# A mixture-of-experts layer: units of four and two token tiles, seven block products in two layers, W1 and W3 fetched per unit

## The chip, the core and the metric

The kernel runs on one core of a Trainium2 chip. A core has five engines that run side by side, each through its own list of instructions in program order, and wait for each other through semaphores: TensorE (matmuls, PE in the profile; PEld is its loading of weights), VectorE (DVE), ScalarE (ACT), GpSimd (POOL, which here issues indirect DMAs) and SyncE (SP, which issues the other DMAs). SBUF is the working memory with 128 partitions, PSUM holds what matmuls accumulate in eight banks, and HBM is the memory outside. The metric is the device time of one execution in microseconds (us). The trace is that of one profiled execution.

## The reference

4096 tokens of 256 numbers each go through a layer of eight experts, of which each token uses the two with the largest gate.

```python
var = jnp.mean(x * x, axis=-1, keepdims=True)
xn = rms_w * (x * jax.lax.rsqrt(var + EPS))
gate = xn @ wg_W + wg_b + (genre_embed @ gg_W + gg_b)
gate_w = jax.nn.softmax(gate, axis=-1)
topk_w, topk_i = jax.lax.top_k(gate_w, TOP_K)
cw = jnp.sum(jax.nn.one_hot(topk_i, E, dtype=x.dtype) * topk_w[..., None], axis=-2)
h1 = jax.nn.relu(jnp.einsum('bsh,ehm->bsem', x, W1) + b1)
h2 = jax.nn.relu(jnp.einsum('bsem,emn->bsen', h1, W2) + b2)
out_e = jnp.einsum('bsen,enh->bseh', h2, W3) + b3
return jnp.einsum('bseh,bse->bsh', out_e, cw)
```

The result is added to x. Everything is 32-bit floating point; W1 is 256 x 512, W2 512 x 512 and W3 512 x 256 for each expert.

## The kernel before

The pairs of a token and one of its experts are sorted into tiles of 128 pairs that share an expert. The first eight tiles (E = 8) hold tokens of the first quarter, one tile for each expert, known early; the rest are placed once the gates of all tokens are known. Of the rest 56 are sure to be there (NSURE), and up to 69 are possible (NREST); these inputs have 59. A *unit* is what one step of the loop works on. Units 0 to 7 are single tiles. Then come 24 units of two tiles with a common expert (NPAIRED), then the single tiles that are left over, of which the last run in a branch that is chosen by the count at run time.

A unit has three layers. For a single tile they are plain matmuls: layer 1 has 8 of 128 columns, layer 2 has 16 of 128, layer 3 has 4 of 256. In a pair the first layer has 8 matmuls of 256 columns (`layer1`), and layer 2 (`layer2_fast`) multiplies in 2 x 2 blocks by seven products in place of eight (the scheme of Strassen in Winograd's form): from the blocks of W2, called w11, w12, w21 and w22, VectorE makes the sums s1 to s4 (`stage_2`), from the blocks of the hidden layer the differences m1 to m4 (`mix`), and TensorE makes seven products of 4 matmuls of 128 columns each (`product`). Three products accumulate onto earlier ones in the bank UB, which ScalarE copies out in between as q1, q2 and q5; VectorE adds the results together (L910, L912, L916) and ScalarE applies bias and ReLU (L900). Layer 3 (`layer3`) has 4 matmuls of 256 columns for each tile. `give` then multiplies with the gate and adds the scaled bias b3 on VectorE (y, L957), and an indirect DMA on GpSimd adds the rows to the output in HBM; each of these additions waits for the one before.

All weights lie in SBUF (w1a, w2a, w3a), loaded in the first 75 us by SP. The expert of a later unit is only known at run time: VectorE loads its number from `ebt` into a register and copies the expert's W1, W2 and W3 to fixed places (st1, st2, st3; `stage_1`, `stage_2`, `stage_3`). `scaled` makes bc = gate x b3 on VectorE for the later units. The tokens of a unit are gathered by GpSimd two units ahead, stored to a scratch buffer in HBM (`stow`), read back reordered (`shuffle`) and turned by VectorE (`transpose_x`).

The order of every engine's instructions is that of the program text (a schedule written by hand). `step` puts layer 1 of a unit in front of layer 3 of the unit before it, and layer 2 (`step_end`) behind that. In the first seven steps (`head_step`) the routing work of `rest`, a generator that yields the nanoseconds of each piece, is handed out in portions by `more`; its result are the tables idxR (which token stands where) and ebt (which expert a tile has).

Of the kernel before, what the change touches and what calls it, by code (L numbers as in the profile page):

```python
# [9 lines left out]
F32 = mybir.dt.float32  # L10
# [11 lines left out]
def kernel(  # L22
# [41 lines left out]
    NPAIRED = (NSURE - E) // 2  # L64
# [34 lines left out]
    w1a = wall.tile([P, E, HC, M], F32, name="w1a")  # L99
    w2a = wall.tile([P, E, MC, M], F32, name="w2a")  # L100
    w3a = wall.tile([P, E, MC, H], F32, name="w3a")
# [3 lines left out]
    hid = wall.tile([P, 4, MC, BT], F32, name="hid")  # L105
# [69 lines left out]
    gTs = buf(gx, [P, TPB * P], "gTs")  # L175
# [22 lines left out]
    def turned(n):  # L198

        if n < 4:  # L200
            return hid[:, n].rearrange("p c t -> p (c t)")
        return bigf[:, 2 * TPB * H + (n - 4) * TPB * P :][:, 0 : TPB * P]
# [185 lines left out]
    def load_weights(e, parts=(0, 1, 2)):  # L388
        for k in parts:
            dst, src = (  # L390
                (w1a[:, e], W1[e].rearrange("(p c) m -> p c m", c=HC)),
                (w2a[:, e], W2[e].rearrange("(c p) n -> p c n", p=P)),
                (w3a[:, e], W3[e].rearrange("(c p) h -> p c h", p=P)),
            )[k]
            loads.append(nc.sync.dma_start(dst, src))
# [100 lines left out]
    def other_loads():  # L496
# [15 lines left out]
        for e in range(3, E):  # L512
            load_weights(e)
# [42 lines left out]
    def rest():  # L556
# [8 lines left out]
        for _ in pB.choose(None):  # L565
# [6 lines left out]
        more, mm, two, one, base, endp, ends, endt, delta, offs = (  # L572
            te(a) for a in ("more", "mm", "two", "one", "base", "endp", "ends", "endt", "delta", "offs")
        )
        nb_i, np_i = te("nb_i", I32), te("np_i", I32)
        V.tensor_tensor(totA, totA1[:, 1:], totA1[:, 0:E], ALU.subtract)
# [5 lines left out]
        V.tensor_scalar(np_i, nb_i, 0x7FFFFFFE, None, ALU.bitwise_and)  # L582
        V.tensor_copy(one, nb_i)
        V.tensor_copy(two, np_i)
        V.tensor_tensor(one, one, two, ALU.subtract)
        V.tensor_scalar(two, two, float(BT), None, ALU.mult)
        V.tensor_tensor_scan(endp, ones[:, 0:E], two, 0.0, ALU.mult, ALU.add)
        V.tensor_scalar(one, one, float(BT), None, ALU.mult)
        V.tensor_tensor(base, endp, two, ALU.subtract)
        V.tensor_tensor_scan(ends, ones[:, 0:E], one, 0.0, ALU.mult, ALU.add)  # L590
        V.tensor_tensor(offs, base, more, ALU.add)
        yield 2600
        V.tensor_scalar(endt, ends, endp[:, E - 1 : E], None, ALU.add)
        V.scalar_tensor_tensor(offs, pB.adj, -1.0, offs, ALU.add, ALU.add)
        V.tensor_tensor(delta, endt, one, ALU.subtract)
        V.tensor_tensor(delta, delta, endp, ALU.subtract)
        V.tensor_scalar(nex, endt[:, E - 1 : E], 1.0 / BT, float(-NSURE), ALU.mult, ALU.add)
        yield 900

        def place(part):  # L600

            slot, odd = part.slot, part.pre[:, 0]
            V.tensor_tensor(odd, slot, part.along(endp), ALU.is_ge)
            yield 400
            V.tensor_tensor(odd, odd, part.along(delta), ALU.mult)
            yield 400
            V.tensor_tensor(slot, slot, odd, ALU.add)
            yield 400
# [58 lines left out]
        for b in range(E, E + 4):  # L667
            gather(b)
# [7 lines left out]
        eb, eb2 = sa, sb  # L676
        ebc = gTs[:, 0 : NREST * (E - 1)].rearrange("p (t e) -> p t e", e=E - 1)
        for dst, end in ((eb, endp), (eb2, endt)):
            V.tensor_tensor(
                ebc,  # L680
                iot.unsqueeze(2).to_broadcast([P, NREST, E - 1]),
                end[:, 0 : E - 1].unsqueeze(1).to_broadcast([P, NREST, E - 1]),
                ALU.is_ge,
            )
            yield 750
            V.tensor_reduce(dst, ebc, AX.X, ALU.add)
            yield 750
        V.tensor_tensor(eb, eb, eb2, ALU.add)
        V.tensor_scalar(eb2, iot, endp[:, E - 1 : E], float(1 - E), ALU.is_ge, ALU.mult)
        V.tensor_tensor(ebt, eb, eb2, ALU.add)  # L690
        yield 600

# [4 lines left out]
    FIRST = E + NPAIRED  # L697

    def tiles(u):

        if u < E:
            return [u]
        if u < FIRST:
            return [E + 2 * (u - E), E + 2 * (u - E) + 1]
        return [E + 2 * NPAIRED + u - FIRST]

# [22 lines left out]
    cgR = buf(run, [P, E, E], "cg")  # L729

    def gather_cw(u):
        for b in tiles(u):
            cg = cgs[b] = cgR[:, b % E]
            fetch(cg, (cwdA if b < E else cwdR)[:, :], b)

    xT = buf(run, [P, HC, 2, BT], "xT")
    shs = gTs.rearrange("p (s k f) -> p s k f", s=2, k=P // SQ)
# [6 lines left out]
    def shuffle(u):  # L744

        for b in tiles(u):
            for g in range(P // SQ):
                nc.sync.dma_start(
                    shs[ts(g, SQ), b % 2],
# [3 lines left out]
    def transpose_x(u):  # L753
        if u > E:
            for b in tiles(u):
                V.transpose(
                    xT[:, :, b % 2, :].rearrange("p c (k b) -> p k c b", b=SQ),
                    shs[:, b % 2].rearrange("p k (a c) -> p k c a", a=SQ),
                )
            return  # L760
        bs = tiles(u)
        w = len(bs)
# [5 lines left out]
        nc.scalar.copy(xT[:, :, bs[0] % 2 : bs[0] % 2 + w, :], tp)  # L768


    st1 = bigf[:, 0 : HC * M].rearrange("p (c m) -> p c m", c=HC)
    st3 = bigf[:, HC * M : HC * M + MC * H].rearrange("p (c h) -> p c h", c=MC)
# [380 lines left out]
```

## Time and profile before

| | |
|---|---|
| time, median of 3 runs | 496.41 us (495.8 to 496.49) |
| time of the profiled execution | 496.23 us, span 494.5 us |
| TensorE, VectorE, ScalarE, GpSimd busy | 97%, 71%, 40%, 59% of the span |
| from the first pair's layer 1 to the first later single's | 88.7 to 402.8 us |
| bytes moved | 59.36 MB, mean 120 GB/s; 386 GB/s in the head, about 80 in the pair steps |

In a row of a timeline the columns are the start in us, the duration in us (of all the merged instructions), engine, line and operation, the operands as output<-inputs, and the number of instructions; brackets hold the idle time before it and what ended it. SPq is SP's queue of DMAs. In the waits a row says who waited for whom, and then how long in total, how often, and the longest. A row's duration is longer than the distance to the next row's start on the same engine where the two overlap.

### The profile page before, as it was taken

To read this page: it belongs to the slowest core of one execution; us is meant where nothing else is said; L and a number is where in the kernel's file an instruction comes from. 1 tells how busy PE (TensorE), PEld (TensorE's weight loads), DVE (VectorE), ACT (ScalarE), POOL (GpSimd) and SP (SyncE) were. 2 spreads that over 40 slices of the span, in tenths; PEclk is the share of its full clock that TensorE was granted. 3 is DMA by queue.
4 is the path that set the end of the run, shared out by engine and by line. 5 is a ranking of instruction groups with operands and counts; after the bars stand their busy time and mean duration, and the time that the engine had idled before them with its cause. 6 is when DMAs were issued, how large, how long until landed. Compare 5 with 4: busy or idle time off the path is not lost. (4 is left out here: it accounts for less than half of the span.)

```text
span 494.5 us, 10440 instructions
## 1 busy us (share of the span) xinstructions
PE 479.9 (97%) x3416; PEld 449.5 (91%) x3416; DVE 351.9 (71%) x875; ACT 196.9 (40%) x514; POOL 291.5 (59%) x229
## 2 busy tenths in 40 slices
PE   7899999999999999999999999999999999999991
PEld 5689999999999999999999999999999999999991
DVE  5796996677877777777777777788777765565540
ACT  5744434344333444433333333433334434344430
POOL 3356326776666665656666666666666556765631
PEclk9999999999999999999999999999999999999997
DMA  8599998444434443434444434444444333433201
GB/s 328 190 368 386 385 385 293 84 110 85 82 78 76 87 72 76 81 73 86 84 86 88 80 77 82 81 87 81 79 83 76 66 66 66 89 66 69 45 3 24
DMA packets 68265, 59.36 MB, mean 120 GB/s; under 512 B 39615, under 2 KB 59298, under 8 KB 67812
## 3 DMA queue, kind: packets, MB, share of 16 engines
q1 hardware_dynamic: 52608, 41.21, 25.6%
q0 software_dynamic: 15232, 17.34, 22.0%
q8 instruction: 29, 0.48, 0.4%
q14 instruction: 40, 0.33, 0.2%
q10 hardware_dynamic: 356, 0.01, 0.0%
HBM read 42.80 MB, written 20.71 MB: 128 GB/s over the span
## 5 line engine op out<-in xcount | busy, mean ns | idle before, releaser
L961 POOL DMA_INDIRECT out_dram<-y,idxR x59 | 107.4, 1821 | 110.0 <-DVE big L820 26.6
L874 PE MATMUL pb<-xT,big 128*128 128x256 f32 (+1 forms) x560 | 108.3, 346 | 0.0
L948 PE MATMUL pb<-big,hid 128*128 128x256 f32 x472 | 107.6, 379 | 0.0
L874 PEld LDWEIGHTS pb<-xT,big 128*128 128x128 f32 x560 | 91.7, 191 | 8.7
L948 PEld LDWEIGHTS pb<-big,hid 128*128 128x128 f32 x472 | 88.8, 190 | 11.6
L883 PE MATMUL pb<-hotA,big 128*128 128x128 f32 x768 | 97.5, 275 | 0.0
L883 PEld LDWEIGHTS pb<-hotA,big 128*128 128x128 f32 x768 | 91.5, 192 | 0.0
L712 POOL DMA_INDIRECT big<-in_x_dram,idxR x59 | 76.1, 1290 | 20.9 <-issue 15.5
L712 POOL DMA_INDIRECT cg<-cwdR,idxR x59 | 65.5, 1110 | 18.0 <-issue 17.7
L877 ACT ACTIVATE hid<-pb,bb 128x256 f32<-128x256 f32 (+1 forms) x140 | 61.2, 439 | 31.6 <-PE pb L874 27.9
L900 ACT ACTIVATE hid<-hid,bb 128x128 f32<-128x128 f32 (+1 forms) x96 | 38.4, 447 | 49.9 <-DVE hid L912 45.4
L883 PE MATMUL pb<-hid,big 128*128 128x128 f32 x384 | 50.7, 275 | 0.0
L883 PEld LDWEIGHTS pb<-hid,big 128*128 128x128 f32 x384 | 48.6, 192 | 1.2
L904 ACT COPY iotx<-pb 128x256 f32<-128x256 f32 x24 | 8.9, 372 | 91.0 <-PE pb L883 91.0
L910 DVE TENSOR_TENSOR hid<-pb,iotx 128x256 f32<-128x256 f32 x24 | 10.2, 425 | 44.7 <-PE pb L883 44.7
L932 PEld LDWEIGHTS pb<-hid,big 128*128 128x128 f32 x352 | 41.0, 192 | 0.6
L932 PE MATMUL pb<-hid,big 128*128 128x128 f32 x352 | 41.1, 275 | 0.0
L957 DVE SCALAR_TENSOR_TENSOR y<-pb,cw,bc 128x256 f32<-128x256 f32 x59 | 28.3, 480 | 14.6 <-PE pb L948 14.6
L935 ACT ACTIVATE hid<-pb,bb 128x128 f32<-128x128 f32 x44 | 16.1, 367 | 43.9 <-PE pb L932 43.9
L932 PEld LDWEIGHTS pb<-hid,w2a 128*128 128x128 f32 x256 | 29.9, 192 | 1.1 <-issue 0.8
L932 PE MATMUL pb<-hid,w2a 128*128 128x128 f32 x256 | 30.7, 276 | 0.0
L961 POOL DMA_INDIRECT out_dram<-y,idxA x8 | 14.9, 1867 | 23.3 <-DMA out_dram<-in_x_dram 7.3
(248 smaller groups left out, 621.2 us busy)
## 6 DMA issues: line engine op xcount, KB each, us to landing
w2a<-in_L_cond_W_dram SPq DMA_DIRECT2D x8, 1024.0 KB
scr<-big SPq DMA_DIRECT2D x57, 128.0 KB
gTs<-scr SPq DMA_DIRECT2D x228, 32.0 KB
w1a<-in_L_cond_W_dram SPq DMA_DIRECT2D x8, 512.0 KB
w3a<-in_L_cond_W_dram SPq DMA_DIRECT2D x8, 512.0 KB
out_dram<-in_x_dram SPq DMA_DIRECT2D x4, 768.0 KB
big<-in_x_dram SPq DMA_DIRECT2D x4, 512.0 KB
big<-in_x_dram SPq DMA_DIRECT2D x2, 1024.0 KB
```

The source lines that it names most:

```text
L712: return nc.gpsimd.indirect_dma_start(out=dst, out_offset=None, in_=src, in_offset=bass.IndirectOffsetOnAxis(ap=index(b), axis=0), bounds_ ...
L874: nc.tensor.matmul(ph, lhsT=w1[:, c, ts(m, P)], rhs=cols[:, c, :], start=(c == 0), stop=(c == HC - 1))
L877: nc.scalar.activation(hids[:, 0, m, 0 : w * BT], ph, AF.Relu, bias=bb[:, 0, m : m + 1])
L883: nc.tensor.matmul(bank[:, ts(n, BT)], lhsT=w[:, k, ts(n, P)], rhs=h[:, k], start=fresh_bank and n == 0 and k == 0, stop=n == HB - 1 and k ...
L900: nc.scalar.activation(hids[:, 1, n, cols], src, AF.Relu, bias=bb[:, 1, n : n + 1])
L904: nc.scalar.copy(q1, UB)
L910: V.tensor_tensor(half(1, 0, 0), tall(AB), tall(q1), ALU.add)
L932: nc.tensor.matmul(ph, lhsT=w2[:, m, ts(n, P)], rhs=hids[:, 0, m, 0 : w * BT], start=(m == 0), stop=(m == MC - 1))
L935: nc.scalar.activation(hids[:, 1, n, 0 : w * BT], ph, AF.Relu, bias=bb[:, 1, n : n + 1])
L948: nc.tensor.matmul(po, lhsT=hids[:, 1, n, ts(k, BT)], rhs=w3[:, n, :], start=(n == 0), stop=(n == MC - 1))
L957: V.scalar_tensor_tensor(y, sums(b), cw, bc, ALU.mult, ALU.add)
L961: add = nc.gpsimd.indirect_dma_start(out=orows, out_offset=bass.IndirectOffsetOnAxis(ap=index(b), axis=0), in_=y, in_offset=None, bounds_c ...
```

## The change

- **Units.** Of the sure tiles behind the first eight, 32 go into eight units of four tiles (NQ), 16 into eight units of two (NP), and the rest are single. The pairs come first in time, then the units of four, then the singles. The routing gets a third level of positions (`part`, `end`, `delta`; `place` runs twice), and `ebt` needs three comparisons.
- **Layers 1 and 2 of both kinds by seven products** (class `Fast`, l = 0 for layer 1, l = 1 for layer 2). A product of layer 1 has 2 matmuls and one of layer 2 has 4, of 128 columns in a pair and 256 in a unit of four. Layer 1 gets sums of W1's blocks (`fold`) and differences of x (`mix`) on VectorE too. `p(k)` makes product k, whereby products 6, 7 and 4 accumulate in the bank U after 1, and 3 in the bank X after 5. c11, c12 and c22 are VectorE's additions; r1, r22 and r21 are the ReLUs. c22 reads U before product 4 is added to it.
- **Order.** `step_fast` weaves products 3 and 4 of layer 2 of the unit before (`before`) and its layer 3 between the products of layer 1.
- **W1 and W3** have three places each (`w1r`, `w3r`), filled from HBM on SP: for the later units by the expert's number, which SP loads into a register (`stream_1` two units ahead, `stream_3` one); for experts 3 to 7 by `load_weights` in the head, as places come free. W1 and W3 aren't copied in SBUF any more, W2 is.
- **bc** is made by ScalarE in `step_fast`, with a register load there (`scaled`, `expert`); the gates' columns cw are copied by VectorE earlier (`scales`). There are four buffers for y and bc each, and layer 3 uses both halves of its two banks.

```diff
-    NPAIRED = (NSURE - E) // 2
+    NQ = (NSURE - 3 * E) // 4
+    NP = (NSURE - E - 4 * NQ) // 2
...
+            for k in range(1, len(masks)):
+                V.tensor_tensor(odd, slot, part.along(end[k - 1]), ALU.is_ge)
+                yield 400
+                V.tensor_tensor(odd, odd, part.along(delta[k]), ALU.mult)
+                yield 400
+                V.tensor_tensor(slot, slot, odd, ALU.add)
+                yield 400
...
+    def stream_1(u):
+        e = expert(u, mybir.EngineType.SP)
+        nc.sync.dma_start(w1r[u % RING], W1[e].rearrange("e (p c) m -> p (e c) m", c=HC))
...
+        def fold(self):
+            a11, a12, a22, s1_, s2_, s3_, s4_ = self.blocks()
+            if self.l:
+                w2e = w2a[:, ex[self.u]].rearrange("p e c m -> p (e c) m")
+                a21 = w2e[:, 0:HB, M2:M]
+                yield
+                V.tensor_copy(up2, w2e[:, :, 0:M2])
+                yield
+                V.tensor_copy(a22, w2e[:, HB:MC, M2:M])
+            else:
+                a21 = ww[self.u][0][:, 0 : HC // 2, M2:M]
+            V.tensor_tensor(s1_, a21, a22, ALU.add)
+            yield
+            V.tensor_tensor(s2_, s1_, a11, ALU.subtract)
+            yield
+            V.tensor_tensor(s3_, a11, a21, ALU.subtract)
+            yield
+            V.tensor_tensor(s4_, a12, s2_, ALU.subtract)
+            yield
...
+            bank, w, x, new = {
+                1: (self.U, a11, b(0, 0), True),
+                2: (self.A, a12, b(1, 0), True),
+                3: (self.X, s4_, b(1, 1), False),
+                4: (self.U, a22, t[3], False),
+                5: (self.X, s1_, t[0], True),
+                6: (self.U, s2_, t[1], False),
+                7: (self.U, s3_, t[2], False),
+            }[k]
...
+    def step_fast(u, last):
+        far = fetches_of(u, last, True)
+        gather_cw(u + 1)
+        f, g = Fast(u, 0), Fast(u, 1)
+        before = Fast(u - 1, 1) if u > E else None
+        staged = g.fold()
+        f.p(1)
+        if before:
+            before.c22()
+            before.r22()
+            before.p(3)
+        next(staged)
+        next(staged)
+        f.p(5)
+        if before:
+            before.c12()
+            before.r1()
+            before.p(4)
+            before.r21()
+        next(staged)
+        f.p(2)
+        f.c11()
+        f.p(6)
+        next(staged)
+        f.p(3)
+        f.c12()
+        f.r1()
+        if u - 1 >= E:
+            scales(u - 1)
+        scaled(u - 1, "A")
+        n = len(tiles(u - 1))
+        first, then, rest_ = {1: ([0], [], []), 2: ([0], [1], []), 4: ([0, 1], [2], [3])}[n]
+        layer3(u - 1, first)
+        give(u - 1, first)
+        for _ in staged:
+            pass
+        g.mix(1)
+        f.p(7)
+        f.c22()
+        f.r22()
+        stage_1(u + 1)
+        if then:
+            layer3(u - 1, then)
+            give(u - 1, then)
+        f.p(4)
+        f.r21()
+        g.mix(2)
+        g.mix(3)
+        fast_next = u + 1 < FIRST
+        nf = Fast(u + 1, 0) if fast_next else None
+        if fast_next:
+            for _ in nf.fold():
+                pass
+        if rest_:
+            layer3(u - 1, rest_)
+        g.mix(4)
+        if rest_:
+            give(u - 1, rest_)
+        transpose_x(u + 1)
+        if far:
+            shuffle(u + 2)
+        if fast_next:
+            for k in (1, 2, 3, 4):
+                nf.mix(k)
+        for k in (1, 5, 6, 2):
+            g.p(k)
+        g.c11()
+        g.p(7)
```

## The prediction

> **What bounds the kernel now.** I read the page first, then the timeline of two pair steps from the middle, then the waits.
>
> ```profile
> span 494.5 us, 10440 instructions
> ...
> PE 479.9 (97%) x3416; PEld 449.5 (91%) x3416; DVE 351.9 (71%) x875; ACT 196.9 (40%) x514; POOL 291.5 (59%) x229
> ...
> PE   7899999999999999999999999999999999999991
> ...
> PEclk9999999999999999999999999999999999999997
> ```
>
> TensorE is busy in every slice but the first two and the last, at full granted clock. So a microsecond of matmuls removed is a microsecond of time, as long as nothing makes TensorE wait. The timeline says whether that holds inside a step:
>
> ```profile
> 203.65 0.97 PEld L883 LDWEIGHTS pb<-hid,iotx 128*128 128x128 f32 x8
> ...
> 204.54 0.97 PEld L883 LDWEIGHTS pb<-hotA,big 128*128 128x128 f32 x8
> ...
> 204.85 0.42 DVE L916 TENSOR_TENSOR hid<-pb,iotx 128x256 f32<-128x256 f32 x1 [0.40 <-PE pb L883]
> 205.19 0.69 DVE L819 COPY big<-w2a 128x1024 f32 x1
> 205.37 0.91 ACT L900 ACTIVATE hid<-hid,bb 128x256 f32<-128x256 f32 x2 [0.19 <-DVE hid L916]
> ...
> 205.54 3.62 PE L874 MATMUL pb<-xT,big 128*128 128x256 f32 x16
> 205.79 0.42 DVE L820 COPY big<-w2a 128x512 f32 x1
> ...
> 206.24 0.69 DVE L821 TENSOR_TENSOR big<-w2a,big 128x512 f32<-128x512 f32 x1
> ...
> 206.97 0.69 DVE L822 TENSOR_TENSOR big<-big 128x512 f32<-128x512 f32 x1
> ...
> 207.58 0.68 DVE L823 TENSOR_TENSOR big<-big,w2a 128x512 f32<-128x512 f32 x1
> ...
> 209.00 3.62 PE L948 MATMUL pb<-big,hid 128*128 128x256 f32 x16
> ```
>
> A record is half of a 32-bit matmul. From 203.65 to 204.54 one block product (4 matmuls of 128 columns, 8 records) takes 0.893: 0.2233 a matmul. From 205.54 to 209.00 layer 1 (8 matmuls of 256 columns) takes 3.455: 0.432 each. Layer 3 takes the same. A pair step is 7 x 0.893 + 3.455 + 3.455 = 13.16, with no gap on TensorE, which is also the distance from one step to the next (V.transpose at 199.89, 213.05, 226.21). In the window of one step VectorE is busy 10.07 of 13.16: today it has some 3 us of air.
>
> ```profile
> ACT iotx L904 <- PE pb L883: 91.0, 24, 3.9
> ...
> DVE hid L910 <- PE pb L883: 44.7, 24, 1.9
> ```
>
> In the waits of the pair steps ScalarE and VectorE wait for TensorE; nothing in these steps shows TensorE waiting for them.
>
> **TensorE work removed.** Layer 1 of a pair goes from 8 x 0.432 to 7 products of 2 matmuls of 128 columns: 14 x 0.2233 = 3.13, so a pair step is 3.13 + 6.25 + 3.455 = 12.83 (-0.33). A unit of four has 14 + 28 + 16 matmuls, all of 256 columns: 58 x 0.432 = 25.05, against 26.32 for two pairs (-1.27). Eight of each: -2.6 - 10.2 = **-12.8**. This is what the change can bring.
>
> **Does TensorE stay fed?** Prices: VectorE starts of one instruction to the next are 0.61 for 512 elements, 0.345 for 256, 0.60 for the copy of 1024, 0.45 for that of 512 (203 to 209 above, and the mixes at 131.69 to 132.91), 0.41 for y, 0.36 a transpose. Estimate for 128 elements, which the trace has only as single instructions of 0.29: 0.21. For 512 from PSUM: the row of 0.69 (L207), next start after 0.62. VectorE or ScalarE start 0.37 after the weight loads of a product have ended (202.75 to 203.13, 213.23 to 213.60). ScalarE starts 0.10 after VectorE's end (205.27 to 205.37), TensorE 0.05 after it (15.02 to 15.07, L342 to L348).
>
> In a pair step VectorE loses the copies of W1 and W3 (0.60 + 0.60) and two bc rows (0.7), and gains four sums of W1 (1.4), four differences of x (0.85) and three additions behind layer 1 (1.05). I sum the new pair step to 11.4 of 12.83. [...]
>
> The sum fits, the order may not. Both engines take their work in program order. In the new step VectorE's order is: c22 of the unit before, up2 copy, its c12, a22 copy, s1, c11, s2, c12, two cw, y0, s3, s4, mix1, **c22**, bb, y1, mix2, mix3, ...; ScalarE's has bc0 behind both ReLUs r1. Product 4 of layer 1 adds into the bank that c22 reads, so TensorE waits for c22, and all of layer 2 is queued behind it. Step time from the first product, pair:
> - TensorE: p1 to 0.45, old p3 1.34, p5 1.79, old p4 2.68. The a22 copy overwrites the weights of old p4: it starts at 3.05.
> - a22 0.45, s1 0.61, c11 0.35, s2 0.61, c12 0.35: 5.42.
> - ScalarE: 0.10 + r1 0.91 (two of 256, above): 6.43; a register load, then bc0 0.515 (L861): 7.15. The load isn't in the trace for ScalarE; VectorE's costs 0.22 (bc to cw 0.27 apart, bc to bb, with a load between, 0.49). Between 0 and 0.4 I take 0.2.
> - VectorE: 0.10, y0 0.41, s3 0.61, s4 0.61, mix1 0.345, c22 0.42: 9.64; TensorE 0.05: p4 at 9.69. Dense, it was due at 7.92: **stall 1.77**. Then p4 and five products of layer 2, 0.45 + 4.47: the pair step is 14.6, not 12.83.
>
> Unit of four: bc is early enough (11.1). y1 waits for the second tile of layer 3, at 11.23 + 0.37; then y1 0.41, s3, s4, mix1 (now 512) 1.83, c22 0.70: 14.6 with the wake, where p4 was due at 13.82: **stall 0.8**, so 25.85. The first pair has no old products to work on while it waits: c12 at 3.2, bc0 at 4.95, c22 at 7.5 where 4.4 was due: 3.0. The first unit of four, with the short steps of a pair before it: c12 8.2, two ReLUs of 512 (estimate 1.5) 9.8, bc0 10.5, c22 13.6 where 10.4 was due: 3.2. Sum: 3.0 + 7 x 1.8 + 3.2 + 7 x 0.8 = **+24.4**.
>
> [...] If c22 could pass the eight instructions in front of it, it would run at 6.35 + 0.37 and no stall be left: 485 by a free order. [...]
>
> **The head.** The third level of units adds six rows of eight elements (0.15 each), three of 192 (0.39) and three of 64 (0.26): +2.9 on VectorE ahead of the first table. The table's first matmuls stand on TensorE at 62.3, its operand is ready at 60.1 and would be at 63.0; the later ones have 1 to 3 us more. I take +1.0, between 0 and 2.9. The expert numbers get three comparisons instead of two and come some 3 us later (81 to about 85); SP waits there with W1 of the first pair behind it, whose sums precede its second product at about 90. I take +0.3, between 0 and 2. Leaving the last unit of four costs 0.3: its ReLUs end just behind the next layer 1. The old loads of experts 3 to 7 now wait for a ring place (layer 1 of three units before), 20 us ahead of use with the queues at 386 GB/s: nothing.
>
> **Weights from HBM.** 1.05 MB a unit on SP, in front of the stow and shuffle of the same step. Today 58 to 82 GB/s move; singles (7.09 us each) would ask for 58 + 148, under the 386 of the head. W1 is asked for two units ahead, W3 is used two units behind its request: at a quarter of the head's rate 0.5 MB lands in 5.4 us, cover 13 or more. Cost 0; were the cover gone, TensorE would stand for the rest of the landing in each unit. POOL's order (gathers, cw, additions) has 10.2 of work in a pair step: nothing. Singles lose two copies on VectorE that nobody waited for (their TensorE is gapless at 7.09): nothing.
>
> **Sum.** Profiled execution 496.2 (span 494.5; median of the runs 496.41): -12.8 + 24.4 + 1.6 = +13.2: **509.4**.
>
> **Rivals.**
> 1. *TensorE stays dense* (the other side): c22 comes before product 4's turn. It needs the chain shorter by 1.77 in a pair and 0.8 in a unit of four; it gains from the point where stalls are under 11 in all. For it: today's steps have no gap. Against: four kinds of rows with measured prices stand between y0 and c22. Time 496.2 - 12.8 + 1.6 = 485. Chance 0.10; half-way, 488 to 495: 0.05.
> 2. *bc0 is not what ends last*: ScalarE's register load is free and y0 waits only for layer 3 (6.3). Then y0 to c22 ends at 8.7, the pair is 13.65, the first of each kind is 0.5 and 1.3 better: 509.4 - 6.7 - 1.8 = 501. Chance 0.22 (with all values from 497.4 to 504).
> 3. *VectorE is the bound of the pairs*: durations instead of starts, or loads and stores colliding. Chain 2.67 and 2.70 instead of 2.37 and 2.40: pair 15.2, units of four 26.3: 509.4 + 8 x 0.6 + 8 x 0.45 = 518. Chance 0.13.
> 4. *The change does not do what it says on the queues*: W1, W3 or the shuffles land late; 1 us in each of 27 units: 530. Against: the head moves 386 GB/s. Chance 0.05.
>
> The likeliest, 504 to 515, has 0.42; the rest (0.03) is no change. A measurement here tells 0.2% (1 us) from nothing. Faster 0.15, same 0.03, slower 0.82. The range 490 to 521 leaves out most of rival 1 and all of 4.
>
> **What would show it.** Pair steps of 14.6 and steps of four of 25.85, start to start; a gap on TensorE in front of layer 1's last product, ended by VectorE's c22; y0 started by ScalarE's bc; head at most 2 us later; TensorE's busy sum lower by some 13. Wrong would be a gap in front of a matmul that waits for w1r or w3r, or pairs under 13.2.

## The result and the profile after

The changed kernel takes 529.91 us (median of 4 runs, 524.67 to 530.77), the kernel before 496.45 us beside it (495.8 to 496.52): a ratio of 1.0655, 95% interval 1.0584 to 1.0726. The profiled run took 530.6 us, span 528.8. The forecast of 509.4 had the sign and missed the size; the time lies outside its range of 490 to 521. (Some executions of a kernel take over 1.5% longer than its fastest, as in run 17 one of 504.29 us at a mean clock of 0.980 beside one of 495.42 at 0.988; medians and spreads below include them, ratios leave them out.)

The page of the changed kernel:

```profile
span 528.8 us, 9839 instructions
...
PE 479.6 (91%) x3032; PEld 434.5 (82%) x3032; DVE 322.2 (61%) x842; ACT 220.8 (42%) x535; POOL 276.2 (52%) x229
...
PE   7899999799999999999999999999999996986692
...
PEclk9999999899999999999999999999999999898997
```

TensorE has 384 records fewer, yet is busy as long as before, where the forecast expected some 13 us less. Matmuls at a lower clock count as busy for longer (some 6 us, last section), and so does part of each step with a wait: a pair step of 14.10 counts 13.11 busy and a unit of four 25.30, where steps without a wait are 12.83 and 25.04 long (4 us in all). The holes are in the last sixth, where the row reads 6986692. That is the stretch of single tiles, which the forecast held to be untouched. By stages (starts of the weight loads of each unit's first layer):

| | before | after | difference |
|---|---|---|---|
| head, to the first pair | 88.72 | 91.02 | +2.3 |
| first pair to the second single | 322.9 | 332.4 | +9.4 |
| second to last single, nine steps | 63.8 | 86.3 | +22.5 |
| last single to the end | 19.1 | 19.1 | 0.0 |

These four are the whole difference of the spans, 34.3. (The second single is the mark because layer 3 of the last unit of four, 6.8 us, lies in the first single's step.)

A pair step from the middle, by the timeline (columns as in the rows before the change):

```profile
154.53 0.42 DVE L986 TENSOR_TENSOR hid<-pb,q1s 128x256 f32<-128x256 f32 x1
...
154.98 0.91 ACT L992 ACTIVATE hid<-hid,bb 128x256 f32<-128x256 f32 x2 [1.13 <-DVE hid L986]
...
155.79 0.89 ACT L869 ACTIVATE bc<-b_sb,cw 128x256 f32 x2
...
156.32 0.48 DVE L1032 SCALAR_TENSOR_TENSOR y<-pb,cw,bc 128x256 f32<-128x256 f32 x1 [1.25 <-ACT bc L869]
...
157.92 0.41 DVE L954 TENSOR_TENSOR hotA<-hid 128x256 f32<-128x256 f32 x1
158.26 0.41 DVE L989 TENSOR_TENSOR hid<-pb,q1s 128x256 f32<-128x256 f32 x1
...
158.72 0.52 PEld L971 LDWEIGHTS pb<-mixX,w1r 128*128 128x128 f32 x4 [1.40 <-DVE hid L989]
```

c12 (L986), r1 (L992), bc (L869), y0 (L1032), mix1 (L954), c22 (L989), product 4: the chain that the prediction wrote down, each started by the one it named. The step is 14.10. Three rows in the waits of the whole kernel are new. The first is the tail, the other two are this chain:

```profile
DVE xT L782 <- DMA gTs<-scr: 40.5, 7, 8.9
...
DVE y L1032 <- ACT bc L869: 22.7, 16, 1.7
...
PEld pb L971 <- DVE hid L989: 21.0, 16, 3.3
```

The last row is product 4 waiting for c22, once in each of the sixteen pairs and units of four. The first is the transpose of the singles' tokens waiting for the read-back. What delays it is in the timeline of the singles, here of the changed kernel (SPq rows are DMAs issued by SP: scr is the store, gTs the read-back):

```profile
448.57 0.36 SPq L828 DMA_DIRECT2D w1r<-in_L_cond_W_dram  x1
...
449.77 0.41 SPq L832 DMA_DIRECT2D w3r<-in_L_cond_W_dram  x1
...
450.26 0.46 SPq L767 DMA_DIRECT2D scr<-big  x1
...
455.37 1.75 SPq L773 DMA_DIRECT2D gTs<-scr  x4
...
458.57 0.45 DVE L782 STREAM_TRANSPOSE xT<-gTs 128x256 f32<-128x256 f32 x1 [6.16 <-DMA gTs<-scr]
```

From the store to the read-back that waits for it 5.1 us pass (450.26 to 455.37), and 4.7 to 5.9 in all six stores from there on. Two loads of 512 KB now stand right ahead of the store. In the kernel before, the seven stores from 417.95 on took 1.7 to 2.7; two of them:

```profile
429.14 0.35 SPq L742 DMA_DIRECT2D scr<-big  x1
430.99 1.73 SPq L748 DMA_DIRECT2D gTs<-scr  x4
...
443.12 0.34 SPq L742 DMA_DIRECT2D scr<-big  x1
445.71 1.73 SPq L748 DMA_DIRECT2D gTs<-scr  x4
```

SP's list now takes 8.9 to 9.5 us from one single's loads to the next (448.57 to 476.20), where TensorE needs 7.09 for a single. On GpSimd of the changed kernel, a few us earlier:

```profile
421.27 1.63 POOL L1033 DMA_INDIRECT out_dram<-y,idxR  x1 [1.33 <-DVE y L1032]
426.31 1.59 POOL L1033 DMA_INDIRECT out_dram<-y,idxR  x1 [3.42 <-DVE xT L782]
430.98 2.46 POOL L1033 DMA_INDIRECT out_dram<-y,idxR  x1 [3.08 <-DMA out_dram<-y,idxR]
436.44 1.59 POOL L1033 DMA_INDIRECT out_dram<-y,idxR  x1 [3.00 <-DMA out_dram<-y,idxR]
438.33 1.69 POOL L736 DMA_INDIRECT big<-in_x_dram,idxR  x1 [0.30 <-issue]
```

The gather of a single's tokens (438.33) stands behind four additions of the last unit of four, each of which waits for the one before. Its tokens reach TensorE at 450.13, after a gap of 5.42.

### The profile page after: what moved, and what is told of

It reads as the page before. It is cut to its first block, busy times and chain, and to the rows that moved or that the text cites. A ratio compares the mean times of both kernels' runs of the same rounds, so it can differ in the third digit from the quotient of the medians.

```text
span 528.8 us, 9839 instructions
## 1 busy us (share of the span) xinstructions
PE 479.6 (91%) x3032; PEld 434.5 (82%) x3032; DVE 322.2 (61%) x842; ACT 220.8 (42%) x535; POOL 276.2 (52%) x229
## 5 line engine op out<-in xcount | busy, mean ns | idle before, releaser
L1020 PE MATMUL pb<-w3r,hid 128*128 128x256 f32 x536 | 125.1, 379 | 0.0
L1020 PEld LDWEIGHTS pb<-w3r,hid 128*128 128x128 f32 x536 | 99.3, 190 | 12.1
L992 ACT ACTIVATE hid<-hid,bb 128x256 f32<-128x256 f32 (+2 forms) x128 | 61.5, 529 | 61.6 <-DVE hid L989 24.8
L971 PE MATMUL pb<-hid,big 128*128 128x128 f32 (+1 forms) x384 | 71.0, 328 | 0.0
L880 PE MATMUL pb<-xT,w1r 128*128 128x128 f32 x304 | 40.6, 291 | 13.9 <-issue 13.9
L1032 DVE SCALAR_TENSOR_TENSOR y<-pb,cw,bc 128x256 f32<-128x256 f32 x59 | 27.9, 475 | 38.0 <-ACT bc L869 21.3
L971 PE MATMUL pb<-mixB,big 128*128 128x128 f32 (+1 forms) x256 | 47.1, 327 | 0.0
L971 PE MATMUL pb<-hotA,big 128*128 128x128 f32 (+1 forms) x256 | 45.9, 335 | 0.0
L890 PE MATMUL pb<-hid,big 128*128 128x128 f32 x352 | 42.6, 281 | 2.8 <-DVE cw L852 2.8
L971 PEld LDWEIGHTS pb<-hotA,big 128*128 128x128 f32 x256 | 40.7, 199 | 3.3
L971 PEld LDWEIGHTS pb<-mixB,big 128*128 128x128 f32 x256 | 40.0, 191 | 3.4
```

The source lines that it names most:

```text
L880: nc.tensor.matmul(ph, lhsT=w1[:, c, ts(m, P)], rhs=cols[:, c, :], start=(c == 0), stop=(c == HC - 1))
L890: nc.tensor.matmul(ph, lhsT=w2[:, m, ts(n, P)], rhs=hid[0][:, m, 0:BT], start=(m == 0), stop=(m == MC - 1))
L971: nc.tensor.matmul(bank[:, ts(n, self.w)], lhsT=w[:, c, ts(n, P)], rhs=x[:, c], start=new and n == 0 and c == 0, stop=n == HB - 1 and c == ...
L992: nc.scalar.activation(out, src, AF.Relu, bias=ww[self.u][1][:, self.l, n : n + 1])
L1020: nc.tensor.matmul(po, lhsT=hid[1][:, n, ts(k, BT)], rhs=w3[:, n, :], start=(n == 0), stop=(n == MC - 1))
L1032: V.scalar_tensor_tensor(y, sums(b), cw, bc, ALU.mult, ALU.add)
```

## The experiments

Three explanations of the 22.5 us were to be told apart: the order of SP (theory A), GpSimd's list (B), the memory traffic as such, whatever the order (C).

**1. The store ahead of the weights.**

```diff
+        if far:
+            stow(u + 2)
         if E + 1 < u + 2 < last + open_end:
             stream_1(u + 2)
         if E < u + 1 < last + open_end:
             stream_3(u + 1)
-        if far:
-            stow(u + 2)
```

> Edit: in each step SP issues the store of the gathered tokens (stow) ahead of the loads of W1 and W3, instead of behind them. Theory A (SP's order): from 450 us on each single step takes 9.0 to 11.8 us because the store's 128 KB stand behind 1 MB of weights and the read-back (shuffle) waits for them; with the store first these six steps come down to 7.1 to 7.8 each and the time to 513 to 519 us. The gap of 5.4 us ahead of 450, which began with a late gather on GpSimd, stays. Theory B (GpSimd's queue of additions is what makes the singles late): nothing changes by more than 3 us, 527 to 531. Theory C (the memory traffic itself is too much, whatever the order): the weights come later in place of the tokens, 525 to 531.

530.49 us, ratio to before 1.0689 (1.0671 to 1.0707): no gain. Read by the total, theory A is dead. Read by stages it is half right. Weight loads of the singles' layer 1:

```profile
444.66 1.87 PEld L880 LDWEIGHTS pb<-xT,w1r 128*128 128x128 f32 x16
...
465.14 3.49 PEld L880 LDWEIGHTS pb<-xT,w1r 128*128 128x128 f32 x16 [13.31 <-issue]
...
474.38 1.87 PEld L880 LDWEIGHTS pb<-xT,w1r 128*128 128x128 f32 x16
...
481.47 1.87 PEld L880 LDWEIGHTS pb<-xT,w1r 128*128 128x128 f32 x16
```

From 474 on every step is 7.1 or 7.5, with the same megabyte of weights in each. But the gap behind the late gather grew from 5.4 to 13.3, and the units of four ended 7.1 later (418.1 for 411.0; three of them took 26.5, 27.9 and 30.3). The waits of pairs and units of four show what by (who waits for whom, total, times, longest):

```profile
DVE y L1032 <- DMA out_dram<-y,idxR: 11.9, 8, 3.3
```

y found its four buffers held by additions not yet done; the changed kernel has no such wait. The gain had been taken back by GpSimd's list, at both ends. The loss in the units of four comes with this edit: run 3, which has it too, shows it again (26.6, 27.7 and 30.5), and run 14, where only the singles' stores go first, does not (25.75). Why GpSimd's list grows longer with it wasn't followed up.

**2 and 3. The singles' gathers one step earlier; and both edits.**

```diff
-        if u + 3 >= FIRST + 2:
+        if u + 3 == FIRST + 3:
+            vs += [u + 3, u + 4]
+        elif u + 3 > FIRST + 3:
+            vs += [u + 3] * (u == CUT) + [u + 4]
+        elif u + 3 == FIRST + 2:
             vs.append(u + 3)
```

> Edit: the gathers of the single tiles are issued one step earlier on GpSimd, so that the gather seen at 438.3 us stands ahead of the last unit of four's four additions (421 to 436). SP's order as in the changed kernel. Theory A (SP's order): only the gap of 5.4 us ahead of 450 goes, singles stay at about 9.1 us: 522 to 526 us. Theory B (GpSimd's backlog is the cause of all of it): singles come back to 7.1 us, 507 to 512.

> Edit: both, the store ahead of the weights on SP and the gathers a step earlier on GpSimd. Theory A: nearly all of the 22.5 us that the nine last single steps lost goes: 507 to 511 us, which is the changed kernel's pairs and units of four with the tail of the kernel before. Theory B gives the same as for the gathers alone, theory C 525 or more.

527.14 us (524.25 to 534.33; ratio 1.0603, 1.0547 to 1.066) and 524.42 (522.19 to 527.45; 1.0553, 1.0523 to 1.0583). The first is not told from the changed kernel's 1.0655, and neither came to the 507 to 512 that theory B gave for the one and theory A for the other. In the second the gap stayed (6.0): VectorE's longest wait there is for the gate columns cw, 10.0 us, whose fetch stood behind the same additions and had not been moved.

**4. No weights for the singles.** These units multiply by what lies in the three places, so their output is not the reference's.

```diff
-        if E + 1 < u + 2 < last + open_end:
+        if E + 1 < u + 2 < FIRST:
             stream_1(u + 2)
-        if E < u + 1 < last + open_end:
+        if E < u + 1 < FIRST:
             stream_3(u + 1)
```

> Edit: the loads of W1 and W3 for the single units are left out; these units multiply by what lies in the three places, so that the output of the singles is not the reference's. Order on SP and GpSimd as in the changed kernel. Theory A (the weights in front of the store) and theory C (traffic) both expect single steps of 7.1 to 7.5 us behind the one gap of 5.4 us that GpSimd makes: 511 to 516 us. Theory B: 527 to 531. If this one is fast and the store-first kernel is not, it is the traffic; if both are, it is the order.

508.81 us (505.82 to 509.07). All singles are 7.1 apart but one (7.84), although four chained additions stand ahead of a gather here too (435.67). So it takes the weights to make the tail late. With the first run it follows that it isn't their bandwidth alone: there the steps from 474 on are 7.1 to 7.5 with all weights in flight, and in the changed kernel only 132 GB/s move between 425 and 490 us, against 394 in the head.

**5. c22 ahead of y0 and mix1.**

```diff
-        give(u - 1, first)
         for _ in staged:
             pass
-        g.mix(1)
         f.p(7)
         f.c22()
         f.r22()
+        give(u - 1, first)
+        g.mix(1)
```

> Edit to the changed kernel: on VectorE the sums s3 and s4, then product 7's c22 and its ReLU stand ahead of y0 and of mix1; nothing else moves. Theory 1 (the stall ahead of product 4 is only c22's place in VectorE's list, as the prediction has it): the 13.4 us of these stalls in the pairs and 7.6 in the units of four go, pairs take 12.8 to 12.9, units of four 24.9 to 25.1, and the time comes to 507 to 511 us. Theory 2 (GpSimd is already full in the units of four: its cycle of gathers, gate columns and four chained additions took 26.6 to 30.8 us, more than their 25.75): the pairs get their 12.9, but y then waits for additions, units of four stay at 26 to 28 us and the last singles as late as they were: 515 to 526 us. Theory 3 (VectorE is full in the pairs): pairs 13.5 or more.

From the third on the pairs are 12.83 to the hundredth, and the wait for c22 is gone from them; theory 1 holds there. The units of four became slower, 26.48 for 25.75, by a stall that this order makes:

```profile
279.60 0.69 DVE L989 TENSOR_TENSOR hid<-pb,q1s 128x512 f32<-128x512 f32 x1 [2.11 <-PE pb L971]
280.21 0.87 DVE L1032 SCALAR_TENSOR_TENSOR y<-pb,cw,bc 128x256 f32<-128x256 f32 x2
...
280.74 1.59 PEld L1020 LDWEIGHTS pb<-w3r,hid 128*128 128x128 f32 x8 [1.58 <-DVE y L1032]
```

Layer 3's third tile waits until y has read its bank, and y now stands behind c22, which waits for product 7. Two later units of four took 27.7 and 31.5: y waits for additions there (24.3 us in eight waits from 320 to 415), as theory 2 had it. The first single came 1.85 us earlier than in the changed kernel, the singles took 8.4 more, and the time is 537.15 (532.76 to 537.67).

**6 to 8. Additions spread; weights behind the read-back; all three.** On GpSimd two of a step's gathers or gate columns go behind each addition, in pairs and units of four (`todo` holds them, `spare(n)` issues n). In run 7 the two `stream` calls move behind `shuffle(u + 2)`; run 8 has the edit of run 5 as well.

```diff
             adds.append(add)
+            spare(2)
...
+        spare(len(todo))
         if far:
+            stow(u + 2)
             shuffle(u + 2)
```

> Edit to the changed kernel: on GpSimd two of a step's gathers or gate columns are issued behind each addition, instead of all of them ahead of the additions, in pairs and units of four; the single tiles are gathered a step earlier. In pairs and units of four the store of the tokens comes behind the weights of the step and right ahead of the read-back. In the singles SP's order is that of the changed kernel (W1, W3, store, read-back). Theory 2 (GpSimd full in the units of four): its cycle drops to about 20 us of work, its backlog at their end and the gap of 5.4 us go, units of four stay at 25.75. The singles stay at about 9.1 us each, since the store still stands behind the weights there: 520 to 526 us. If GpSimd's backlog alone made the singles late: 507 to 511.

> Edit: as the run with the additions spread, and SP issues W1 and W3 of each step behind the read-back instead of ahead of the store. Two causes (GpSimd's backlog, and SP's order in the singles): both are gone, singles 7.1 us each, units of four 25.75, pairs 14.1: 506 to 511 us. If memory traffic as such delays the tokens in the singles: 516 or more.

> Edit: as the run before it, with c22 ahead of y0 and mix1 on VectorE as well. If the three causes add: 21 us less than that run, 485 to 491 us, which is below the kernel before (496.4). If VectorE, or y's buffers, bound the steps then: pairs of 13.4 or more, 493 to 500 us.

534.07, 547.43 and 550.86 us: all worse, mainly in the pairs and at the first unit of four. There the gathers came later than before and the transposes waited for tokens (pairs of up to 16.7 in the first of the three, 18.7 in the second, 24.8 in the third). For the totals these edits were bad ones; they say that the pairs live on gathers that are early.

Run 7's singles missed as well: the last five steps took 8.5 to 12.1, not 7.1. Its SP list holds the best test of theory A, since a step's weights now stand ahead of the next step's store:

```profile
449.38 0.41 SPq L841 DMA_DIRECT2D w3r<-in_L_cond_W_dram  x1
460.06 0.34 SPq L776 DMA_DIRECT2D scr<-big  x1
461.80 1.86 SPq L782 DMA_DIRECT2D gTs<-scr  x4
...
465.15 0.41 SPq L841 DMA_DIRECT2D w3r<-in_L_cond_W_dram  x1
465.99 0.34 SPq L776 DMA_DIRECT2D scr<-big  x1
470.56 1.89 SPq L782 DMA_DIRECT2D gTs<-scr  x4
```

A store 10.7 us behind the last load of weights is read back after 1.7 us, the next one, 0.8 us behind it, after 4.6.

**9 to 12. Mended edits.** For the singles alone, gathers up to five units ahead, gate columns three, both ahead of the additions, and the store ahead of the weights (run 9). With it c22 again, now with s3, s4, y, c22, mix1 in this order (10); or the spreading in the steps behind a unit of four only (11); or all (12).

```diff
-        vs = [u + 2] if u + 2 <= FIRST + 1 else []
-        if u + 3 >= FIRST + 2:
-            vs.append(u + 3)
+        vs = range(FIRST, u + 6) if u >= FIRST - 1 else [u + 2]
...
+        if u >= FIRST - 1:
+            for v in range(u + 1, min(u + 4, last)):
+                if tiles(v)[0] not in cgs:
+                    gather_cw(v)
+        if far and u >= FIRST:
+            stow(u + 2)
...
-        give(u - 1, first)
         for _ in staged:
             pass
-        g.mix(1)
+        give(u - 1, first)
         f.p(7)
         f.c22()
         f.r22()
+        g.mix(1)
...
+    def spread(u):
+        return paired(u) and u > E and len(tiles(u - 1)) == 4
```

> Edit to the changed kernel, for the single tiles alone: on GpSimd their gathers and gate columns are issued up to five and three units ahead, so that none of them stands behind the four additions of the last unit of four; on SP the store comes ahead of W1 and W3 in their steps. Pairs and units of four are issued as in the changed kernel. Theory D (the singles were late by two orders together: gathers and gate columns behind GpSimd's additions, and the store behind the weights on SP): singles 7.1 us each with no gap over 1 us, 506 to 511 us. If the tail is late by memory traffic, singles of 8.5 us or more remain: 518 or more.

> Edit: the run before it, and on VectorE s3 and s4 ahead of y0 (and y1 in units of four), then c22, then mix1: c22 no longer waits behind mix1, and the two y's are no longer behind c22, as they were in the run with c22 first, where layer 3's third tile waited 1.58 us for their bank. Theory: pairs 12.83, units of four 24.9 to 25.1 as long as y's buffers are free. GpSimd's cycle in the units of four was 26.6 to 30.8 us: by it y waits for additions from the fourth or fifth unit of four on, 26.5 to 28 us a unit there: 492 to 503 us in all. If GpSimd is no limit: 485 to 491.

> Edit: the first of these four runs, and in the units of four two gathers or gate columns behind each addition on GpSimd. GpSimd's additions then keep up with y (within 8 us) where they fell behind by up to 20 us; the time doesn't change, 505 to 511 us, since units of four are bound by c22 at 25.75 us.

> Edit: all three, the tail, c22 ahead of mix1 and the additions spread in the units of four. If the causes add up: pairs 12.83, units of four 24.9 to 25.1, singles 7.1: 484 to 490 us, below the kernel before (496.4). If GpSimd's order is no limit it equals the run with tail and c22 alone; if it is, it is 4 us or more faster than that.

556.17, 535.86, 540.09 and 521.43 us; but the kernel before took 504.53 (502.37 to 510.77) beside them, so that only distances within a trace are read here. Pairs that are issued as in the changed kernel took up to 18.4 (run 9). The singles were 7.1 apart in eight of nine steps of runs 11 and 12 and in seven of run 9, and units of four in run 12 were 25.04.

**13 to 15. The changed kernel, the tail edit and all edits once more**, with the kernel before at 496.48.

> The changed kernel itself, unedited, beside the next two on one chip, since the kernel before took 504.5 us in the last four runs where it had taken 496.4 to 496.8. With the kernel before back at 496 to 497: 525 to 531 us, as before. If it is above 502 again, this kernel takes 535 or more.

> The tail edit alone once more (gathers and gate columns of singles ahead of GpSimd's additions, the store ahead of the weights in their steps). Last time its singles were 7.1 us apart, but its pairs and units of four, which are issued as in the changed kernel, took 14.1 to 18.4 and 26 to 31 us. Theory D: on an undisturbed chip pairs 14.1, units of four 25.75, singles 7.1: 507 to 511 us. If the edit itself disturbs the pairs and units of four: 530 or more, beside a changed kernel of 525 to 531.

> Tail, c22 ahead of mix1, and additions spread in the units of four, once more. Undisturbed: pairs 12.83 (last time 13 to 16), units of four 25.04, singles 7.1: 486 to 492 us, faster than the kernel before. If pairs of 12.83 leave the tokens too little time for gather, store and read-back whatever the chip: pairs of 13.5 or more and 495 to 510 us.

534.92 us (527.64 to 541.04), 525.53 (519.21 to 530.63) and 501.32 (499.8 to 506.35). The tail edit alone kept pairs at 14.1 and units of four at 25.75 and made seven of nine single steps 7.1, but brought some 6.6 us (by the ratios, 1.0677 and 1.0545), not 20. Its trace names what was left, again y waiting for the last unit of four's additions:

```profile
424.73 0.48 DVE L1032 SCALAR_TENSOR_TENSOR y<-pb,cw,bc 128x256 f32<-128x256 f32 x1 [4.75 <-DMA out_dram<-y,idxR]
...
430.70 0.48 DVE L1032 SCALAR_TENSOR_TENSOR y<-pb,cw,bc 128x256 f32<-128x256 f32 x1 [5.49 <-DMA out_dram<-y,idxR]
...
432.44 6.42 PEld L890 LDWEIGHTS pb<-hid,big 128*128 128x128 f32 x32 [5.57 <-issue]
```

In the third run, which spreads the additions and also moves c22, that wait is gone: pairs 12.83 (the first two 12.9 and 13.0), units of four 25.04, eight of the nine singles 7.1 or 8.2, the last 13.55. Its GpSimd rows show the additions of the last unit of four 6.7 to 7.1 apart, although all four y's were there by 408; in the run without weights they were 4.5 to 5.5 apart:

```profile
405.42 1.64 POOL L1045 DMA_INDIRECT out_dram<-y,idxR  x1 [2.20 <-DVE y L1044]
412.13 1.60 POOL L1045 DMA_INDIRECT out_dram<-y,idxR  x1 [5.08 <-DVE bb L853]
419.20 1.58 POOL L1045 DMA_INDIRECT out_dram<-y,idxR  x1 [5.47 <-DVE bb L853]
425.85 1.57 POOL L1045 DMA_INDIRECT out_dram<-y,idxR  x1 [5.06 <-DVE bc L879]
```

(The releasers named in the last three are wrong: those VectorE instructions have nothing to do with an addition. What it waits for is the addition before it, as the rows at 430.98 and 436.44 of the changed kernel have it.)

**16 and 17. The last three tiles' gathers ahead of the branch, twice.** In run 15 the gather of the last tile was issued behind the branch and behind additions, at 470.

```diff
-        gs = [lambda b=b: gather(b) for v in ahead(u, last + 2 * open_end) for b in tiles(v)]
+        gs = [lambda b=b: gather(b) for v in ahead(u, last + 3 * open_end) for b in tiles(v)]
```

> Edit: as the run with all causes removed (501.3 us), and the gathers and gate columns of the last three tiles, whose presence is only known at run time, are issued ahead of the branch, which leaves them out of GpSimd's list behind the branch. There the last single began 6.4 us late, since its gather stood behind the additions and was issued at 470 us. Theory (GpSimd's additions, now 6.7 to 7.1 us apart where weights are loaded at the same time, 4.5 to 4.6 where they are not, hold the last gather): the last step takes 7.1 in place of 13.55 us: 491 to 496 us. If the branch itself costs the 6 us: 499 to 503.

> The run before it once more: there the singles were all 7.1 us apart, the last one included, but the kernel before took 505.8 us beside it, and the head and the pairs were late in every kernel. With the kernel before at 496 to 497: head as in the changed kernel, pairs 12.83, units of four 25.04, every single 7.1: 490 to 496 us, at or just below the kernel before.

The first gave 524.1 us with the kernel before at 505.75 beside it; its singles were all 7.1 to 7.3, but from the last single to the end it took 31.0 (19.1 in the changed kernel), with additions up to 9.8 us behind y. The second is the comparison that counts: 498.98 us (495.42 to 504.29, 12 runs) against 496.01 (495.16 to 497.31, 17 runs), ratio 1.0043, interval 1.0017 to 1.007. Of the 33 us that the change cost some 30 are accounted for by edits that only reorder; by stages of the traces 16.8 between the first pair and the second single, which is the chain over c22, and 13.3 behind it, which is the tail. It isn't below the kernel before. Seven of its nine single steps are 7.1, the last two 9.4 and 8.7, and not because of additions:

```profile
456.81 0.40 SPq L844 DMA_DIRECT2D w3r<-in_L_cond_W_dram  x1
...
457.69 1.75 SPq L785 DMA_DIRECT2D gTs<-scr  x4
...
464.96 0.45 DVE L794 STREAM_TRANSPOSE xT<-gTs 128x256 f32<-128x256 f32 x1 [6.59 <-DMA gTs<-scr]
...
465.47 3.39 PEld L892 LDWEIGHTS pb<-xT,w1r 128*128 128x128 f32 x16 [2.24 <-issue]
```

The transpose waits for a read-back that is issued behind two loads of weights, 7.3 us ahead of it, and the 16 weight loads behind the gap take 3.39 us, where those of the singles before it take 1.87. Additions are late only at the end: from the last single on 24.4 us pass, 19.1 in the changed kernel, and the last addition is issued 3.65 us after its y is ready (0.42 there).

**18. No units of four.** 24 pairs, with all edits.

```diff
-    NQ = (NSURE - 3 * E) // 4
+    NQ = 0
```

> Edit: the last version, but with no units of four: 24 pairs in place of eight units of four and eight pairs (the constant NQ is 0, with which the third level of positions goes as well). Pairs are 12.83 us each; the singles then follow a unit with two additions and not four. By the sum: first pair at about 90, pairs to 399, singles 8.8 + 9 x 7.1 to 471.6, end 19.1, 1.7 around the span: 490 to 494 us, below the kernel before (496.0) although a pair of pairs is 0.6 us dearer than a unit of four. If weights for 8 more units, 82 GB/s where units of four need 42, lengthen the additions in the pairs too, or the singles stay as late as in the last version: 497 to 503.

521.75 us, with the kernel before at 507.02 beside it, ratio 1.0206 (1.0123 to 1.0289). The first pair began at 94.0 and several pairs were late (12.83 to 18.4). All nine single steps behind the first were 7.1: without the four chained additions ahead of them the singles are whole, with 21.4 us from the last one to the end. Both of its forecasts were missed (490 to 494, 497 to 503), but the kernel before was late beside it too; whether this version is below 496 with the kernel before at 496 stays open.

## Why the prediction was wrong

| term | forecast | measured |
|---|---|---|
| pair and unit of four without stalls | 12.83, 25.05 | 12.83 (runs 5, 15), 25.04 (run 15) |
| pair step, unit of four | 14.6, 25.85 | 14.10, 25.75 |
| stall of product 4: first pair, first four | 3.0, 3.2 | 3.29, 1.62 |
| head | +1.3 | +2.3 |
| from first pair to second single | +11.9 | +9.4 |
| singles and the end | 0 | +22.5 |

**Right: pairs and units of four.** The removed matmuls are worth what the sum said. The chain over bc0 is the one in the trace, and run 5 shows that it is only VectorE's list: with c22 moved and nothing removed the wait is gone from the pairs. That VectorE takes its list in order, on which the sum rests and without which it put the time at 485, holds in the trace: the weight loads of the product that c22 reads ended at 155.81, and c22 ran at 158.26, behind bc's wait and the four instructions of its list ahead of it (y0 156.32, s3 156.72, s4 157.32, mix1 157.92). What was off is the end of bc: y0 began 6.79 us into the step (149.53 to 156.32), not 7.25. ScalarE's register load, put at 0.2, doesn't show (bc follows r1 without a gap), and one bc takes 0.49 (L869, median), where the sum had 0.515. So a pair loses 1.27 (14.10 for 12.83; the row's 1.40 is the idle time of the weight loads), not 1.77. Rival 2 (y0 waits for layer 3 alone, a pair of 13.65) is wrong: bc0 does end last, by 1.25 us of waiting. Rival 3 (VectorE bounds the pairs) is wrong too: from y0's start to c22's end 2.35 pass (156.32 to 158.67), near the sum's 2.37 and not the 2.67 that durations gave, since the instructions overlap (s3 and s4 of 0.68 start 0.60 apart); VectorE was busy 11.21 of the 14.10, and run 5's pairs take 12.83.

The stage from the first pair to the second single came 2.5 under the sum: 3.4 less in the later pairs, 0.6 in the later units of four and 1.6 in the first of them, against some 3 more in the first pair. There TensorE also waited 1.54 for its second product (93.08; the profile names a ScalarE copy that had ended at 92.14) and later ran at half the clock for 3.4 us (0.52 from 101.70 to 105.10). That product needs VectorE's sums of W1, which began late, after 2.58 us of waiting for the load of W1 (90.94): the one place found where a weight held TensorE up, one of the signs of being wrong that the prediction named. The head's 2.3 are mainly three gaps on TensorE: 1.15 in the routing (63.80), where 1.0 was put, 0.51 for the first pair's gathered tokens (86.84) and 0.29 at its start (91.02).

**Wrong: "Weights from HBM. [...] Cost 0".** The step counted bytes per second and how early each weight is asked for, and found both ample, which they are in the singles: what their matmuls wait for is the transposed tokens. It listed that the loads go "on SP, in front of the stow and shuffle of the same step" and asked only when the *weights* land, never when the *store behind them* lands. That took 1.7 to 2.7 us before and 4.7 to 5.9 after. "Singles [...] nothing" fell with it: +22.5. Run 7 shows both cases in one list: a store 10.7 us behind the last load of weights was read back after 1.7, one 0.8 us behind it after 4.6. The additions, which GpSimd issues, came slower beside the weights too (6.7 to 7.1 apart for 4.5 to 5.5, last section). The runs show these times; why a store behind weights takes longer, and whether both have one cause, was not shown.

**Wrong as well: "POOL's order [...] has 10.2 of work in a pair step: nothing".** It was summed for a pair alone. In a pair one addition in two waits for the one before with nothing to do in between, in a unit of four three in four. In the changed kernel, from first gather to first gather the units of four took GpSimd 26.6, 27.4, 26.7, 30.8 and 29.0 us (230.03, 256.64, 284.01, 310.75, 341.56, 370.57), TensorE 25.75. It fell behind unit by unit, unseen, as y has four buffers, and the bill came with the first singles: the gap of 5.42.

The two don't separate into shares, since each takes over where the other goes: SP's order alone brought nothing (run 1), the singles' gathers alone nothing that stands out of the spread (run 2), both with the gate columns some 6.6 us (run 14, beside run 13), and only with the additions spread as well was the tail nearly whole (runs 12 and 15; both also move c22, and run 11, without it, had eight of nine singles at 7.1). Rival 4 named the queues and, by luck, the time (530), with 0.05: it spread the loss evenly over 27 units, and the pairs and units of four had none of it. Without the tail's 22.5 the changed kernel would be at 508.1, and the run without the singles' weights gave 508.8, beside a forecast of 509.4. That is nearer than the terms were, as the head's 1.0 more and the middle's 2.5 less cancel in part.

**Open:** the gap of 3.21 us at 484, where the engines enter the branch of the last tiles (VectorE goes on 0.29 us ahead of the late read-back there, at 482.87, and 0.25 ahead of it in the kernel before, at 454.39, which suggests that the store is waited for again; no run shows it); what made the kernel before take 501 to 511 us beside runs 9 to 12, 16 and 18, and everything in them late; and what makes up the rest of the last 5 us at the end of run 17.

## What to carry to other kernels

When a transfer is put into a queue, ask what stands behind it and who waits for *that*, not only whether the transfer itself is early enough; do it for the shortest step of the program, not the typical one. When units grow, sum every engine's cycle again for the new unit, the waits of chained DMAs included: an engine that is some 9% too slow (28.1 us a unit where TensorE has 25.75) hides behind buffers and shows much later, somewhere else. And read an experiment by stages: run 1 changed the total by nothing and had repaired the singles' own step.

## What the runs showed of the hardware

**Gaps on TensorE can cost twice.** In the changed kernel's singles, weight loads of layer 1:

```profile
437.54 1.87 PEld L880 LDWEIGHTS pb<-xT,w1r 128*128 128x128 f32 x16
...
450.13 3.29 PEld L880 LDWEIGHTS pb<-xT,w1r 128*128 128x128 f32 x16 [5.42 <-issue]
...
477.62 1.86 PEld L880 LDWEIGHTS pb<-xT,w1r 128*128 128x128 f32 x16 [2.01 <-issue]
```

After 5.42 us 16 loads take 3.29 instead of 1.87, after 2.01 nothing is lost. By stretches (us, busy time of PE, PEld, DVE, ACT and POOL, granted clock, DMA share, GB/s) the clock is halved for 3.4 us and whole again:

```profile
449.75:453.15 3.40, 2.99 (x14) 3.02 (x15) 2.39 (x6) 0.73 (x2) 2.79 (x3) 0.50 0.80 249
453.20:456.20 3.00, 3.00 (x22) 2.79 (x21) 0.00 (x0) 0.69 (x2) 2.39 (x3) 1.00 0.81 196
```

The same follows the gaps of 3.29 us (first pair, clock 0.52 from 101.70 to 105.10), 3.21 (0.55 from 484.21 to 487.60) and 4.67 (0.52 from 501.07 to 504.47); the four cost 1.3 to 1.7 each on top, some 6 us of the 34. No term of the forecast had it. The runs show no sharp border: a gap of 2.24 was enough in run 17 (465.47, 3.39 for 16 loads), while after one of 2.20 in the changed kernel (468.45) 16 loads took 1.86, and after one of 3.63 in run 7 (202.40) 4 loads took 0.52, as in a step without a gap.

**Chained additions to HBM took 4.5 to 7.1 us each.** In run 4, with no singles' weights in flight, the last unit of four's were 4.5 to 5.5 apart; in the changed kernel, where SP stood still from 430 to 443, 4.7 to 5.5; in run 15, with a megabyte of weights in every 7 us, 6.7 to 7.1, at 129 and 177 GB/s in the two slices of its page there, two fifths of the head's rate (395). No run varied the traffic at these additions alone.
